# Expert routing of batches 2 to 7: turned on VectorE and moved by DMA, with TensorE, ScalarE and VectorE in a fixed order and the expert weights begun by GpSimd

## The chip, the cores and the metric

The kernel runs on one core of a Trainium2 chip. The metric is device time in microseconds (us) of one execution: 1364.11 us before, the median of three runs (1360.69 to 1366.95).

## The reference, cut to what matters

Eight batches of 256 tokens with 256 channels pass through two layers, all in float32. The changed part is the feed-forward of the first layer, a soft mixture of 8 experts with 128 slots each:

```python
xn = rmsnorm(x, norm_gamma);  sn = rmsnorm(slot_embeds, slot_norm_gamma)
logits   = einsum('bnd,esd->bnes', xn, sn)        # 256 tokens x 1024 slots per batch
dispatch = softmax(logits, axis=1)                # over the tokens
combine  = softmax(logits.reshape(b, n, e*s), axis=-1)   # over the slots
slots = einsum('bnd,bnes->besd', xn, dispatch)
h  = gelu(einsum('besd,edh->besh', slots, w1) + b1)      # 256 -> 1024
eo = einsum('besh,ehd->besd', h, w2) + b2                # 1024 -> 256
out = einsum('bmd,bnm->bnd', eo.reshape(b, e*s, 256), combine)
```

Before it stands a cross-attention with 16 heads of 16, behind it one with 16 heads of 64, and a gated channel mix ends the kernel.

## The kernel before

**Stages.** One program holds the first cross-attention (to about 286 us by the timeline), the expert phase (286.47 to 913.3), the second cross-attention and the channel mix. PSUM is shared out in three kinds of tile: `big`, two of 128x1024; `mm`, three of 128x512; `o`, one of 128x512.

**Experts.** The batches go in four groups of two (`experts(g)`, L951). An expert has eight pieces, one per 128 hidden columns: `up(e, hc)` (L957) is two matmuls into half of a `ph` tile, followed by a gelu on ScalarE (L976) into `ht`. The even and the odd piece share one `ph` tile. After each `up` a `down(e - 1, k)` (L979) of the expert before is issued: two matmuls of `ht` by `w2`, accumulated in `pe`. A matmul in float32 shows as two records on TensorE, so each `up` and each `down` is 4 records. The last `down` of an expert is followed on VectorE by the addition of `b2`, which leaves the expert's output in its `slots` tile (L993). `combine` (L1007) sums the eight outputs with the token weights `CT`, and scales by `rzn`.

**Routing.** While group g is in its experts, the routing of group g + 1 (`routing(g + 1)`, L804) and the combines of group g - 1 run as side pieces: a list `side`, from which one is taken after each odd piece from the tenth on (`n % 2 == 1 and n > 8`). For each batch there are

- `prepare`: normalised tokens `xh`, four transposes on TensorE, `xnT`;
- `by_token(t)`: logits `ln` of a half of the tokens by the 1024 slots (L832), the negated maximum on VectorE (L840), the exp with its sum on ScalarE into `en` (L843), and two copies of the logits into `lg` (L850);
- `turn_token(t)`: eight transposes of `en` on TensorE into `ptn` (L858), and copies into `CT` (L863);
- `by_slot(q)`: eight transposes of `lg` into `ls` in PSUM (L873), the maximum, four exps into `es` (L884), a multiplication by the reciprocal sums on GpSimd (L892);
- `turn_slot(q)`: eight transposes of `es` into `pts` (L902), copies into `dt`;
- `fill(q)`: `pf` = `xh` by `dt` (L914), scaled by `gam` into the `slots` tiles of the next group.

Routing of batches 0 and 1 stands in the first cross-attention (`routing0`) and works in its own way.

**Order.** The stages outside use helpers, `matmul` and `transpose` (L71 to L76), that hand the instruction to `tc.keep_in_program_order`; such instructions stand on their engine in the order of the code. In the expert phase plain `nc.tensor.matmul` and `nc.scalar.activation` are used, and a scheduler sets their order at build time by its own estimates.

**Weights.** `load_expert` (L217) issues `w1` (1 MB), `w2` (1 MB) and `b2` of one expert from SyncE, at the expert's first piece; two sets of tiles take turns (`moe_sets[e % 2]`). The first set is issued late in the first loads, at 30.30 us.

Of the kernel before, what the change touches and what calls it, by code (L numbers as in the profile page):

```python
# [14 lines left out]
P = 128  # L15
# [47 lines left out]
def kernel(ctx: ExitStack, tc: tile.TileContext, a: dict, out: bass.AP):  # L63
# [153 lines left out]
    def load_expert(to, e):  # L217
        nc.sync.dma_start(to["w1"], a["w1"][e].rearrange("(c p) f -> p c f", p=P))
        nc.sync.dma_start(to["w2"], a["w2"][e].rearrange("(c p) f -> p c f", p=P))
        nc.sync.dma_start(to["b2"], a["b2"][e].partition_broadcast(P))  # L220

    moe_sets = [moe_tiles(pr, 0)]
    with ExitStack() as l0:
# [550 lines left out]
        at(50, lambda: load_expert(set0, 0))  # L774
# [25 lines left out]
    with ExitStack() as l0f:  # L800
        pm = l0f.enter_context(tc.tile_pool(name="pm", bufs=2))
        moe_sets.append(moe_tiles(l0f.enter_context(tc.tile_pool(name="po", bufs=1)), 1))

        def routing(g):  # L804
# [7 lines left out]
            steps = []  # L812
            for bl in range(2):
# [3 lines left out]
                def prepare(b=b, st=st):  # L817
                    st["xh"] = normed(b, mv, scl, "moe", of=4)
                    pt = transposed(st["xh"], f"xm_{b}")
                    xnT = pm.tile([P, 2, S], F32, tag="xnT", name=f"xnT_{b}")  # L820
                    for c in range(2):
                        nc.vector.tensor_scalar(
                            xnT[:, c, :], pt[:, c, :], gam[:, c : c + 1], None, ALU.mult
                        )
                    st["xnT"] = xnT

                def by_token(t, b=b, bl=bl, st=st):

                    pl = ps_big(f"ln_{b}_{t}")
                    for m in range(2):  # L830
                        for c in range(2):
                            nc.tensor.matmul(  # L832
                                pl[:, m * 512 : (m + 1) * 512],
                                lhsT=st["xnT"][:, c, t * P : (t + 1) * P],
                                rhs=snT[:, c, m * 512 : (m + 1) * 512],
                                start=(c == 0),
                                stop=(c == 1),
                            )
                    nm = stat.tile([P, 4], F32, tag="nm", bufs=4, name=f"nmn_{b}_{t}")
                    nc.vector.tensor_reduce(nm[:, 0:1], pl, AX.X, ALU.max, negate=True)  # L840
                    en = pm.tile([P, 1024], F32, tag="em", bufs=4, name=f"en_{b}_{t}")
                    z = stat.tile([P, 4], F32, tag="zm", bufs=4, name=f"zn_{b}_{t}")
                    nc.scalar.activation(  # L843
                        en, pl, AF.Exp, bias=nm[:, 0:1], accum_out=z[:, 0:1]
                    )
                    nc.vector.reciprocal(rzn[:, 2 * bl + t : 2 * bl + t + 1], z[:, 0:1])
                    st[f"en{t}"] = en
                    for m in range(2):
                        lg = pm.tile([P, 512], F32, tag="lg", bufs=6, name=f"lg_{b}_{t}_{m}")
                        nc.vector.tensor_copy(lg, pl[:, m * 512 : (m + 1) * 512])  # L850
                        st[f"lg{t}{m}"] = lg

                def turn_token(t, b=b, bl=bl, st=st):
                    for m in range(2):
                        pt = ps_mm(f"ptn_{b}_{t}_{m}")
                        for i in range(4):
                            e = 4 * m + i
                            nc.tensor.transpose(  # L858
                                pt[:, i * P : (i + 1) * P],
                                st[f"en{t}"][:, e * P : (e + 1) * P],  # L860
                                ident,
                            )
                        nc.vector.tensor_copy(  # L863
                            CT[:, bl, 4 * m : 4 * m + 4, t * P : (t + 1) * P],
                            pt.rearrange("p (e n) -> p e n", e=4),
                        )

                def by_slot(q, b=b, st=st):

                    pl = ps_big(f"ls_{b}_{q}").rearrange("p (i n) -> p i n", i=4)  # L870
                    for i in range(4):
                        for t in range(2):
                            nc.tensor.transpose(  # L873
                                pl[:, i, t * P : (t + 1) * P],
                                st[f"lg{t}{q}"][:, i * P : (i + 1) * P],
                                ident,
                            )
                    nm = stat.tile([P, 4], F32, tag="nm", bufs=4, name=f"nms_{b}_{q}")
                    nc.vector.tensor_reduce(nm, pl, AX.X, ALU.max, negate=True)
                    es = pm.tile([P, 1024], F32, tag="em", bufs=4, name=f"es_{b}_{q}")  # L880
                    es = es.rearrange("p (i n) -> p i n", i=4)
                    z = stat.tile([P, 4], F32, tag="zm", bufs=4, name=f"zs_{b}_{q}")
                    for i in range(4):
                        nc.scalar.activation(  # L884
                            es[:, i, :],
                            pl[:, i, :],
                            AF.Exp,
                            bias=nm[:, i : i + 1],
                            accum_out=z[:, i : i + 1],
                        )  # L890
                    nc.vector.reciprocal(z, z)  # L891
                    nc.gpsimd.tensor_tensor(  # L892
                        es, es, z.unsqueeze(2).to_broadcast([P, 4, S]), ALU.mult
                    )
                    st[f"es{q}"] = es

                def turn_slot(q, b=b, st=st):
                    dt = pm.tile([P, 2, 512], F32, tag="dt", bufs=2, name=f"dt_{b}_{q}")
                    for t in range(2):
                        pt = ps_mm(f"pts_{b}_{q}_{t}")  # L900
                        for i in range(4):
                            nc.tensor.transpose(  # L902
                                pt[:, i * P : (i + 1) * P],
                                st[f"es{q}"][:, i, t * P : (t + 1) * P],
                                ident,
                            )
                        nc.vector.tensor_copy(dt[:, t, :], pt)
                    st[f"dt{q}"] = dt

                def fill(q, b=b, bl=bl, st=st):  # L910
                    for c in range(2):
                        pf = ps_mm(f"pf_{b}_{q}_{c}")
                        for t in range(2):
                            nc.tensor.matmul(  # L914
                                pf,
                                lhsT=st["xh"][:, t, c * P : (c + 1) * P],
                                rhs=st[f"dt{q}"][:, t, :],
                                start=(t == 0),
                                stop=(t == 1),
                            )  # L920
# [9 lines left out]
                steps.append([prepare])  # L930
                for t in range(2):
                    steps.append([lambda f=by_token, t=t: f(t), lambda f=turn_token, t=t: f(t)])
                for q in range(2):
                    steps.append(
                        [
                            lambda f=by_slot, q=q: f(q),
                            lambda f=turn_slot, q=q: f(q),
                            lambda f=fill, q=q: f(q),
                        ]
                    )  # L940
            pieces = []
            depth = max(len(s) for s in steps)
            for n in range(len(steps) + depth - 1):
                for k in range(depth):
                    if 0 <= n - k < len(steps) and k < len(steps[n - k]):
                        pieces.append(steps[n - k][k])
            return pieces, CT, rzn
# [3 lines left out]
        def experts(g):  # L951
# [5 lines left out]
            def up(e, hc):  # L957
                if hc == 0:
                    w = moe_sets[e % 2]
                    if g or e:  # L960
                        load_expert(w, e)
                    cur[e] = dict(w1=w["w1"], w2=w["w2"], b2=w["b2"], ht=[])
# [4 lines left out]
                for c in range(2):  # L967
                    nc.tensor.matmul(  # L968
# [7 lines left out]
                nc.scalar.activation(ht, ph, AF.Gelu, bias=b1[:, e, hc : hc + 1])  # L976
                c_["ht"].append(ht)

            def down(e, k):  # L979
# [3 lines left out]
                for hc in range(2 * (k % 4), 2 * (k % 4) + 2):  # L983
                    nc.tensor.matmul(  # L984
# [22 lines left out]
        def combine(g, bl, t, eos, CT, rzn):  # L1007
            pc = ps_mm(f"pc_{g}_{bl}_{t}")
            for e in range(E):
                nc.tensor.matmul(  # L1010
# [30 lines left out]
        for g in range(4):  # L1041
# [3 lines left out]
            if g < 3:  # L1045
                if g == 2:
                    moe_mean(3)
                    moe_scale([3])
                pieces, CT, rzn = routing(g + 1)
                side += pieces  # L1050
            for n, piece in enumerate(work_):
                piece()
                if n % 2 == 1 and n > 8 and side:
                    side.pop(0)()
# [464 lines left out]
```

## Time and profile before

| | |
|---|---|
| median of 3 runs | 1364.11 us |
| the profiled execution | 1366.39 us |
| its span in the trace | 1364.6 us |
| granted TensorE clock, mean | 0.989 |
| the expert phase | 286.47 to 913.3 us, 626.8 us |

The profile is one execution on the chip. PE is TensorE's matmul, PEld its weight load, DVE is VectorE, ACT is ScalarE, POOL is GpSimd, SP is SyncE, which here only issues DMAs. The first part of the page gives for each engine the busy microseconds, the share of the span and the number of instructions; matmuls are pipelined, and their ends are modelled, so busy times on PE overlap a little and start-to-start times are the better measure. The chain is followed back from the last instruction, at each step to what released it. A group is a line, an engine and an operation with its tiles (out<-in), a count, the busy time, the mean nanoseconds of one, and behind the last bar the idle time of the engine just before and what ended most of it. In the timeline a row has its start, its length, engine, line and operation, and in brackets the idle time before it. The duration of a merged row (x4, x8) covers all its instructions.

### The profile page before, as it was taken

How to read it: one execution, taken by the hardware profiler on the slowest of the kernel's cores; microseconds unless marked ns; L12 is line 12 of the kernel's file. 1: busy time of each engine (PE TensorE's matmuls, PEld its weight loads, DVE VectorE, ACT ScalarE, POOL GpSimd, SP SyncE). 2: the span in 40 equal slices, each digit the busy share in tenths (PEclk: the TensorE clock that was granted, in tenths of full speed). 3: DMA queues.
4: the chain of work that ended last, by engine and by line, in shares of the span. 5: the costliest groups of instructions: out<-in, count | busy, mean ns of one | idle time of the engine just before them, and what ended most of it. 6: DMA issues, size and time to landing. Idle time of an engine off the chain costs nothing.

```text
span 1364.6 us, 18968 instructions
## 1 busy us (share of the span) xinstructions
PE 1324.8 (97%) x7504; PEld 958.8 (70%) x7504; DVE 571.0 (42%) x1160; ACT 582.0 (43%) x1403; POOL 192.8 (14%) x142
## 2 busy tenths in 40 slices
PE   7998999899999999999999999999999999999998
PEld 3565565467678877778777788875666676677777
DVE  6577776523331133321333110015445444544565
ACT  2455444626342164522545222213536445444663
POOL 1000001101010000100001000002333323323433
PEclk8999998999999999999999999999999999999999
DMA  7100000023243324233233324450000000000001
GB/s 219 57 1 2 1 1 1 1 97 132 66 132 131 127 71 131 93 106 130 80 117 131 111 87 153 144 150 1 1 1 1 1 1 1 1 1 1 2 8 54
DMA packets 59128, 86.84 MB, mean 64 GB/s; under 512 B 3360, under 2 KB 49056, under 8 KB 59040
## 3 DMA queue, kind: packets, MB, share of 16 engines
q1 hardware_dynamic: 58464, 85.11, 19.2%
q8 instruction: 59, 0.97, 0.3%
q10 hardware_dynamic: 576, 0.52, 0.1%
q14 instruction: 29, 0.24, 0.1%
HBM read 83.53 MB, written 2.10 MB: 63 GB/s over the span
## 4 chain that ended last, share of the span: by engine, by line
PE 87%; ACT 6%; DVE 5%; issue 1%; DMA 0%; POOL 0%; ACTq 0%; SPq 0%; DVEq 0%; POOLq 0%
PE ph L968 16%; PE pe L984 16%; PE sc L73 8%; PE q L73 6%; PE o L73 5%; PE k L73 5%; PE po L73 5%; PE pc L1010 4%; PE pe L76 4%; PE v L73 4%; PE pf L914 3%; PE ln L832 3%; ACT ex L1222 2%; PE pf L73 1%; ACT ex L501 1%; DVE NM L490 1%
## 5 line engine op out<-in xcount | busy, mean ns | idle before, releaser
L976 ACT ACTIVATE ht<-ph,b 128x256 f32<-128x256 f32 x256 | 119.1, 473 | 372.1 <-PE ph L968 371.7
L968 PE MATMUL ph<-slots,w 128*128 128x256 f32 x1024 | 266.9, 384 | 0.9 <-ACT ht L976 0.2
L984 PE MATMUL pe<-w,ht 128*128 128x256 f32 x1024 | 263.3, 381 | 0.0
L968 PEld LDWEIGHTS ph<-slots,w 128*128 128x128 f32 x1024 | 182.3, 189 | 54.5 <-ACT ht L976 21.8
L984 PEld LDWEIGHTS pe<-w,ht 128*128 128x128 f32 x1024 | 192.0, 190 | 29.9 <-DVE slots L993 4.3
L1235 POOL TENSOR_TENSOR ex<-ex,rz 128x1024 f32<-128x1024 f32 x64 | 120.1, 1897 | 224.2 <-DVE rz L1233 214.0
L1222 ACT ACTIVATE ex<-sc,nm 128x256 f32<-128x256 f32 x256 | 117.2, 483 | 45.5 <-DVE nm L1217 45.5
L501 ACT ACTIVATE ex<-sc 128x512 f32<-128x512 f32 x128 | 74.7, 596 | 86.6 <-PE sc L73 76.1
L73 PE MATMUL sc<-KT,QT 17*128 17x256 f32 (+1 forms) x1024 | 105.3, 385 | 2.1 <-ACT QT L445 1.5
L490 DVE TENSOR_REDUCE NM<-sc 128x2 f32<-128x512 f32 x128 | 86.6, 687 | 41.4 <-PE sc L73 36.9
L993 DVE TENSOR_TENSOR slots<-pe,b 128x512 f32<-128x512 f32 x32 | 22.1, 691 | 185.4 <-PE pe L984 185.4
L73 PE MATMUL q<-xT,wq 128*128 128x256 f32 x384 | 94.8, 395 | 0.9 <-ACT V L1187 0.9
L73 PEld LDWEIGHTS sc<-KT,QT 17*128 17x128 f32 (+1 forms) x1024 | 77.4, 189 | 25.4 <-issue 15.9
L73 PEld LDWEIGHTS q<-xT,wq 128*128 128x128 f32 x384 | 70.9, 192 | 26.4 <-issue 12.9
L892 POOL TENSOR_TENSOR es<-es,zs 128x1024 f32<-128x1024 f32 x12 | 22.7, 1892 | 445.6 <-DVE zs L891 445.6
L1217 DVE TENSOR_REDUCE nm<-sc 128x4 f32<-128x1024 f32 x64 | 75.3, 1218 | 6.5 <-PE sc L73 2.8
L73 PE MATMUL po<-wo,ot 128*128 128x256 f32 x320 | 72.5, 382 | 0.0
L76 PE MATMUL pe<-ident,ex 128*128 128x128 f32 x512 | 69.9, 278 | 0.5 <-DVE xT L1137 0.4
L73 PEld LDWEIGHTS po<-wo,ot 128*128 128x128 f32 x320 | 60.1, 190 | 10.9 <-issue 3.2
L1251 ACT COPY et<-pe 128x512 f32<-128x512 f32 x64 | 37.0, 607 | 71.9 <-PE pe L76 71.5
L76 PEld LDWEIGHTS pe<-ident,ex 128*128 128x128 f32 x512 | 56.2, 140 | 14.0 <-issue 8.0
L73 PE MATMUL o<-et,V 128*64 128x256 f32 x512 | 62.8, 386 | 0.9 <-ACT ot L1270 0.9
(194 smaller groups left out, 1636.8 us busy)
## 6 DMA issues: line engine op xcount, KB each, us to landing
w<-in_w_dram SPq DMA_DIRECT2D x64, 1024.0 KB, 7.0
b<-in_b_dram SPq DMA_DIRECT2D x32, 128.0 KB, 6.8
x_sb<-in_x_dram SPq DMA_DIRECT2D x3, 512.0 KB, 7.3
ctx0T<-in_ctxT_dram SPq DMA_DIRECT2D x4, 256.0 KB, 8.4
ctx1T<-in_ctxT_dram SPq DMA_DIRECT2D x8, 128.0 KB, 6.9
se<-in_slots_dram SPq DMA_DIRECT2D x1, 1024.0 KB, 5.7
wq<-in_wq_dram SPq DMA_DIRECT2D x1, 1024.0 KB, 4.9
wo<-in_wo_dram SPq DMA_DIRECT2D x1, 1024.0 KB, 14.9
```

What stands on the lines that cost most here:

```text
L73: tc.keep_in_program_order(nc.tensor.matmul(out, lhsT=lhsT, rhs=rhs, start=start, stop=stop))
L76: tc.keep_in_program_order(nc.tensor.transpose(out, in_, ident))
L490: nc.vector.tensor_reduce(NMs[(2 * b + t // 2) % 2][:, qb, t, HD0 + 1 + 64 * i : 64 * i + 64 : 32], sc[i][:, :, 0, :], AX.X, ALU.max, nega ...
L501: nc.scalar.activation(ex[:, 2 - 2 * i : 4 - 2 * i, :], sc[1 - i][:, :, 1, :], AF.Exp)
L832: nc.tensor.matmul(pl[:, m * 512 : (m + 1) * 512], lhsT=st["xnT"][:, c, t * P : (t + 1) * P], rhs=snT[:, c, m * 512 : (m + 1) * 512], star ...
L968: nc.tensor.matmul(ph, lhsT=c_["w1"][:, c, hc * P : (hc + 1) * P], rhs=slots[e][:, c * 256 : (c + 1) * 256], start=(c == 0), stop=(c == 1),)
L976: nc.scalar.activation(ht, ph, AF.Gelu, bias=b1[:, e, hc : hc + 1])
L984: nc.tensor.matmul(c_["pe"][:, b, :], lhsT=c_["ht"][hc][:, b * SL : (b + 1) * SL], rhs=c_["w2"][:, hc, :], start=(hc == 0), stop=(hc == HI ...
L1010: nc.tensor.matmul(pc[:, :D], lhsT=CT[:, bl, e, t * P : (t + 1) * P], rhs=eos[e][:, bl, :], start=(e == 0), stop=(e == E - 1),)
L1217: nc.vector.tensor_reduce(nm, sc, AX.X, ALU.max, negate=True)
L1222: nc.scalar.activation(ex[:, i, qb, :], sc[:, i, qb, :], AF.Exp, bias=nm[:, i, qb : qb + 1], accum_out=z[:, i, qb : qb + 1],)
L1235: nc.gpsimd.tensor_tensor(ex, ex, rz.rearrange("p h q -> p (h q)").unsqueeze(2).to_broadcast([P, 4, S]), ALU.mult,)
```

## The change

For groups 1 to 3 (batches 2 to 7):

1. The 48 transposes of each batch on TensorE (`turn_token`, `by_slot`, `turn_slot`) and the 12 copies that follow them or save the logits are gone. In their place VectorE transposes 32x32 blocks (`turn`, and the two in `turn_slot`) into a tile of squares, `tk`, and `spread` moves the blocks to the partitions where they belong: 16 DMAs of 32 partitions (64 KB) on SyncE, three times per batch (logits into `ls`, `en` into `CT` in runs of 128 bytes, the dispatch weights into `dt`). `prepare`'s four transposes stay.
2. The softmax over the tokens reads and writes `ls` in SBUF, not PSUM.
3. The two exps over slots of a batch are issued together, behind the second half's maximum.
4. `tc.keep_in_program_order` (through `matmul` for TensorE) now holds the expert and routing matmuls, the gelus, the exps, the maxima of `by_slot` and the block transposes.
5. The side pieces have a written plan with gaps (`-`), and one is taken after each odd piece from the first on in groups 0 to 2. The four first steps of the next routing come ahead of the combines.
6. The weights are issued by GpSimd: `w2` and `b2` at the expert's first piece, `w1` of the next expert at its second. The first set is issued at the start.
7. `em`, `ls` and `dt` have fewer buffers.

```diff
-    def load_expert(to, e):
-        nc.sync.dma_start(to["w1"], ...)
-        nc.sync.dma_start(to["w2"], ...)
-        nc.sync.dma_start(to["b2"], ...)
+    def load_first(to, e):
+        nc.gpsimd.dma_start(to["w1"], ...)
+    def load_second(to, e):
+        nc.gpsimd.dma_start(to["w2"], ...)
+        nc.gpsimd.dma_start(to["b2"], ...)
...
+        def turn(tk, t, table):
+            for m in range(2):
+                square = nc.vector.transpose(
+                    tk[:, :, t, 4 * m : 4 * m + 4, :].rearrange("p k e x -> p e k x"),
+                    table[:, m * 512 : (m + 1) * 512].rearrange("p (e k x) -> p e k x", e=4, k=4),
+                )
+                tc.keep_in_program_order(square)
+
+        def spread(tk, to, rows="p t e x -> p t (e x)"):
+            for k in range(4):
+                for a in range(4):
+                    nc.sync.dma_start(
+                        to(32 * k, a), tk[32 * a : 32 * a + 32, k, :, :, :].rearrange(rows)
+                    )
...
+                    if t == 1:
+                        st["exp0"]()
+                        exp()
+                    if t == 0:
+                        st["tk_l"] = squares(f"l_{b}")
+                    turn(st["tk_l"], t, pl)
+                    if t == 1:
+                        ls = pm.tile([P, 8, E, 32], F32, tag="ls", bufs=1, name=f"ls_{b}")
+                        st["ls"] = ls
+                        spread(st["tk_l"], lambda k, a: ls[k : k + 32, a::4, :, :].rearrange("p t e x -> p t (e x)"))
...
-                def turn_token(t, b=b, bl=bl, st=st):
-                    for m in range(2):
-                        pt = ps_mm(f"ptn_{b}_{t}_{m}")
-                        for i in range(4):
-                            nc.tensor.transpose(pt[:, i * P : (i + 1) * P], ...)
-                        nc.vector.tensor_copy(CT[:, bl, 4 * m : 4 * m + 4, t * P : (t + 1) * P], ...)
+                def turn_token(b=b, bl=bl, st=st):
+                    tk = squares(f"n_{b}").rearrange("p k t e x -> p k (t e x)")
+                    tk = tk.rearrange("p k (e t x) -> p k t e x", t=2, x=32)
+                    for t in range(2):
+                        turn(tk, t, st[f"en{t}"])
+                    spread(tk.rearrange("p k t e x -> p k e t x"), ...)
...
-                    pl = ps_big(f"ls_{b}_{q}").rearrange("p (i n) -> p i n", i=4)
-                    for i in range(4):
-                        for t in range(2):
-                            nc.tensor.transpose(pl[:, i, t * P : (t + 1) * P], ...)
+                    ls = st["ls"][:, :, 4 * q : 4 * q + 4, :]
...
+            first = [piece(step) for step in ("P0", "T00", "T01", "P1")]
             pieces = []
+            for step in (
+                ("A0 - -" if g == 1 else "A0") + " S00 - S01 T10 - C0 T11 A1 - - F00 F01 S10 - S11 - C1 - - - F10 F11"
+            ).split():
+                pieces.append(piece(step))
+            return first, pieces, CT, rzn
...
+                if hc == 0 and n > 0:
+                    load_second(w, e)
+                if hc == 1 and n < 4 * E - 1:
+                    load_first(moe_sets[(e + 1) % 2], (e + 1) % E)
...
-                nc.scalar.activation(ht, ph, AF.Gelu, bias=b1[:, e, hc : hc + 1])
+                tc.keep_in_program_order(
+                    nc.scalar.activation(ht, ph, AF.Gelu, bias=b1[:, e, hc : hc + 1])
+                )
...
-                pieces, CT, rzn = routing(g + 1)
-                side += pieces
+                first, pieces, CT, rzn = routing(g + 1)
+                side = first + side + pieces
             for n, piece in enumerate(work_):
                 piece()
-                if n % 2 == 1 and n > 8 and side:
+                if n % 2 == 1 and (n > 8 or g < 3) and side:
                     side.pop(0)()
```

The letters of the plan are P `prepare`, T `by_token`, A `turn_token`, S `by_slot`, C `turn_slot`, F `fill`; the first digit is the batch of the pair, the second the half.

## Prediction

> **What bounds the kernel now.** I read the page first: engine busy times, then the chain that ended last.
>
> ```profile
> PE 1324.8 (97%) x7504; PEld 958.8 (70%) x7504; DVE 571.0 (42%) x1160; ACT 582.0 (43%) x1403; POOL 192.8 (14%) x142
> PE 87%; ACT 6%; DVE 5%; issue 1%; DMA 0%; POOL 0%; ACTq 0%; SPq 0%; DVEq 0%; POOLq 0%
> ```
>
> TensorE bounds it. The change lies in the expert phase, which by the timeline runs from 286.47 (first `ph` matmul) to 913.3, 626.8 us, with PE busy 625.95 at clock 1.00, DVE 152.9, ACT 232.4, POOL 22.8. So one microsecond of PE work saved is worth one microsecond, *unless the order opens a wait*. What PE waits for is in the groups, and the transposes that go are in the groups by form:
>
> ```profile
> L976 ACT ACTIVATE ht<-ph,b 128x256 f32<-128x256 f32 x256 | 119.1, 473 | 372.1 <-PE ph L968 371.7
> L968 PEld LDWEIGHTS ph<-slots,w 128*128 128x128 f32 x1024 | 182.3, 189 | 54.5 <-ACT ht L976 21.8
> L873 PE MATMUL ls<-ident,lg 128*128 128x128 f32 x96 | 13.4, 273 | 0.0
> L902 PE MATMUL pts<-ident,es 128*128 128x128 f32 x96 | 12.4, 273 | 0.0
> L858 PE MATMUL ptn<-ident,en 128*128 128x128 f32 x96 | 12.4, 273 | 0.0
> ```
>
> The one thing PE waits for is the gelu (L976): an odd `up` writes the second half of the PSUM tile whose first half the even gelu still reads. The timeline shows this beside an exp:
>
> ```profile
> 313.00 0.47 ACT L976 ACTIVATE ht<-ph,b 128x256 f32<-128x256 f32 x1 [2.17 <-PE ph L968]
> 313.49 1.28 ACT L843 ACT_TABLE_LOAD   x1
> 313.61 1.05 PE L968 MATMUL ph<-slots,w 128*128 128x256 f32 x4
> 314.50 1.03 PE L984 MATMUL pe<-w,ht 128*128 128x256 f32 x4
> 314.79 1.12 ACT L843 ACTIVATE en<-ln,nmn 128x1024 f32<-128x1024 f32 x1
> 315.36 1.04 PE L858 MATMUL ptn<-ident,en 128*128 128x128 f32 x8
> 315.80 0.19 ACT L843 ACTIVATION_READ_ACCUMULATOR en<-ln,nmn 128x1 f32 x1
> 316.01 1.28 ACT L976 ACT_TABLE_LOAD   x1
> 316.31 1.56 PE L984 MATMUL pe<-w,ht 128*128 128x256 f32 x6
> 317.31 0.47 ACT L976 ACTIVATE ht<-ph,b 128x256 f32<-128x256 f32 x1
> 317.83 0.73 PEld L968 LDWEIGHTS ph<-slots,w 128*128 128x128 f32 x4 [0.36 <-ACT ht L976]
> ```
>
> ACT is away from gelus for 3.84 us (table, exp, table). The scheduler fills that time with eight transposes and six `down` matmuls moved forward, and PE loses 0.36. The exps over tokens take longer:
>
> ```profile
> 322.34 0.47 ACT L976 ACTIVATE ht<-ph,b 128x256 f32<-128x256 f32 x1 [1.05 <-PE ph L968]
> 322.83 1.28 ACT L884 ACT_TABLE_LOAD   x1
> ...
> 326.07 1.28 ACT L976 ACT_TABLE_LOAD   x1
> 327.37 0.84 ACT L976 ACTIVATE ht<-ph,b 128x256 f32<-128x256 f32 x2
> ```
>
> From 322.81 to 327.37 no gelu starts: 4.56 us.
>
> **What goes.** 288 transposes. Eight in a row take 0.87 to 0.95 us start to start (315.36 to 316.31 is the longer), so 31.3 to 34.2; the rows' busy sum is 38.2, but busy times overlap. I take 31.3. With 0.217 us per `ph`/`pe` record (four in 0.867), 0.43 per 512-wide record and 3.46 per combine, the phase holds 615.5 of PE work; so 626.8 - 615.5 = 11.3 are waits now. About 0.27 per expert, 8.6 over 32, is the even-gelu pattern away from any exp. It stays; the other 2.7 are counted anew below. Work left: 584.2.
>
> **What the fixed order adds.** In the built program's order PE is even `up`, `down`, odd `up`, `down`, side piece, with nothing moved across, and ACT goes gelu(odd), exps, gelu(next even). The piece S (exps over tokens) has no PE work any more. After the slot boundary PE has `up` and `down`, 1.73 us; the gelu before the exps ended 0.13 ahead of the boundary, so the next ends at -0.13 + 4.56 + 0.47 = 4.90 and PE resumes at 4.95. **Stall 3.2 us, times 12 = 38.4.** Where an S's data come late it is longer: S00 of groups 1 and 2 waits some 1.6 us for the moved logits (twice), in group 0 the reduce of S00 stands behind expert 0's add (+1.0) and that of S10 likewise (+2.25); 6.45 in all. S: 44.9.
>
> The piece T has 3.43 us of PE work per token half. Both exps now run after the second half's reduce (1.22 us) at 3.43 + 0.2 + 1.22 = 4.85; the second exp ends at 6.1, the table load at 7.4, the gelu at 7.9; PE is ready at 5.17. Stall 2.8, five times 13.9. The sixth, in group 0's first expert, has no `down`s beside it: 2.0 for the gelu table (a load at 287.57 and a gelu, less one `up`), 0.78 in each of two pieces whose gelu has no `down` to hide behind, and 2.8 + 0.87 for the missing `down`: 7.2. T: 21.1. In before each T filled itself with transposes. Six table pairs are saved on ACT, which I count inside these sums.
>
> The square root of the next layer's statistics takes a table pair too, some 2.15 each for three groups and 1.7 for the last scale: 8.2.
>
> Phase: 584.2 + 8.6 + 44.9 + 21.1 + 8.2 = **667.0, 40.2 more.**
>
> **What moves off PE.** 60 block transposes on DVE: the nearest rows are 0.714 us for 128x512 from PSUM and 0.436 for 128x256 from SBUF, and 12 of the 60 are 128x1024, so 51 to 55 us on an engine busy 153 of 627; 72 copies (0.64 each, 46 us) go. Hidden by PE, except where one stands ahead of an S reduce (the lateness above).
>
> 288 DMAs from SBUF to SBUF, 64 KB each, on SP. SP's issue costs
>
> ```profile
> 24.12 4.10 SPq L280 DMA_DIRECT2D wo<-in_wo_dram  x8
> ```
>
> 0.51 us each, 8.2 for a spread's sixteen, plus 2.1 to land (those eight landed after 2.3): 10.2 us. No trace here has SBUF to SBUF with 128-byte runs; records of 256 bytes take 18 ns, so 512 runs over 16 engines are 0.58 per DMA, about the issue. Below: 8.2, the issue alone. Above: lane j+8 waits for lane j, two landings of the slowest kind on the page, 14.9 each: 30. I take 10.2, nearest to the 32 KB row. Between first exps and S00 in group 0 stand 5.6 us more than that, between the slot softmax's spread and its fill (C0 to F00) 8, for C1 to F10 0.4 in group 0 and 6 later, and the CT spread must land within 14 before the piece queued behind it asks. So at 10.2 it costs only the 1.6 counted.
>
> Weights leave SP for POOL, in two parts, each a piece earlier or later. A 1 MB load lands 7.0 us after its issue (page); first use is 7 and 8 pieces of 1.73 us later, 12.1 and 13.9. POOL has two 1.9 us multiplications per batch in the phase ahead of them: no cost. The first set moves from 30.3 us to about 4 us, where 2.2 MB share the DMA with the first loads (slice one: 219 GB/s); 2.2 MB at that rate would be 10 us, and the chain there has 0.6 us of slack. Bounds 0 and 10; I take 1, since the loads ahead were issued first.
>
> [...]
>
> Sum: the profiled execution took 1366.4 (span 1364.6); + 40.2 + 1 = 1407.6. The median of the three runs is 2.3 below it: **1405 us**.
>
> **Rivals.**
> - *Faster, 1330 to 1345.* The even gelu isn't late, because the exps start before the slot boundary or the odd `up` isn't held by the shared tile: then an exp block costs under 1 us and the transposes are gained: 1364 - 31.3 - 2.7 + 0 to 15. For it: PE waits only 11 us today with twelve more table pairs. Against: today's cover is `down`s and transposes that the scheduler moved, and the fixed order moves none. It decides if the stall per block (12 S, 6 T, 4 square roots) is under (31.3 + 2.7)/22, about 1.5 us, instead of 3.
> - *No change, about 1368.* Stalls at S as worked out but nothing late, none at T and the square root, whose matmuls cover them as now: 584.2 + 8.6 + 38.4 = 631.2, 4.4 more. For it: T has 3.43 us of matmuls of its own. Against: both exps stand behind them.
> - *Much slower, 1420 to 1450.* Spreads take 20 us instead of 10: S00 then comes some 5 late in group 0 and 10 in the others, the fills 2 to 6: about 6 per batch, 36. It decides from 16 us per spread; speaking for it, each has 512 runs of 128 bytes.
>
> **How the numbers follow.** Forecast 0.70 (1380 to 1425, the stall per block between 2 and 4 us), faster 0.13, no change 0.07, much slower 0.10. The range 1368 to 1435 leaves out the faster case and the far end of the slower. Measurement tells 0.5% (6.8 us) from no change: faster 0.13, same 0.07, slower 0.80.
>
> **What would show it.** No `ptn`, `ls`, `pts` groups on PE; L968's load idle behind ACT up from 22 to some 95 us; PE empty for 3 us after each block of four exps, in the timeline; the phase about 667 long; chain share of ACT up by 4 to 5 points. Wrong if the phase is under 627, if PE's idle is put down to a DMA (the spreads), or if the stages before 286 and after the phase moved.

## The result, and the profile after

The changed kernel took 1452.62 us (median of four, 1446.23 to 1458.04) against 1362.72 for the kernel before (1360.69 to 1366.95): ratio 1.0654, 95% interval 1.0601 to 1.0707. It is slower, as forecast, but by 89.9 us and not by 41; the time lies above the range, which ended at 1435.

These are lines of the page of the changed kernel: busy time of the engines, the granted clock in 40 slices, the chain by engine, and the groups of the `up`s (their matmuls and their weight loads).

```profile
PE 1332.4 (92%) x7216; PEld 956.2 (66%) x7216; DVE 569.2 (39%) x1148; ACT 570.2 (39%) x1391; POOL 262.7 (18%) x238
PEclk9999999998989998989989899999999999999999
PE 74%; ACT 10%; DVE 6%; DMA 5%; SPq 3%; issue 2%; POOL 0%; DVEq 0%; ACTq 0%; POOLq 0%
L73 PE MATMUL ph<-slots,w 128*128 128x256 f32 x1024 | 289.4, 408 | 71.8 <-ACT ht L1021 71.7
L73 PEld LDWEIGHTS ph<-slots,w 128*128 128x128 f32 x1024 | 198.1, 202 | 130.7 <-ACT ht L1021 94.8
```

The clock row and the same group of matmuls in the kernel before:

```profile
PEclk8999998999999999999999999999999999999999
L968 PE MATMUL ph<-slots,w 128*128 128x256 f32 x1024 | 266.9, 384 | 0.9 <-ACT ht L976 0.2
```

PE has 288 instructions fewer and is yet busy for 7.6 us more. That is the line to stop at: the work shrank by 31 us, so what is left must have run slower. The mean of one `ph` record rose from 384 to 408 ns, and the clock row shows dips between slices 10 and 23, in the expert phase, where before it was level. The wait for the gelu is where the prediction put it: PEld's idle time behind ACT is 94.8 us, and ACT's share of the chain went from 6% to 10%.

What one block of exps does is in the timeline of the changed kernel, PE alone (start, length, operation, and in brackets the idle time before):

```profile
414.63 1.03 PE L73 MATMUL ph<-slots,w 128*128 128x256 f32 x4
415.50 1.03 PE L73 MATMUL pe<-w,ht 128*128 128x256 f32 x4
419.73 2.07 PE L73 MATMUL ph<-slots,w 128*128 128x256 f32 x4 [3.21 <-ACT ht L1021]
421.60 1.91 PE L73 MATMUL pe<-w,ht 128*128 128x256 f32 x4
423.30 1.91 PE L73 MATMUL ph<-slots,w 128*128 128x256 f32 x4
425.01 1.46 PE L73 MATMUL pe<-w,ht 128*128 128x256 f32 x4
426.31 1.03 PE L73 MATMUL ph<-slots,w 128*128 128x256 f32 x4
```

The pause is 3.21 us, as long as forecast (3.37 in the account below, which counts from the end of the work and not from the modelled end of the record). But behind it the same four records start 1.70 us apart (421.60 to 423.30) instead of 0.87 (414.63 to 415.50), for some 6.5 us. The table of windows gives the reason; its column behind POOL is the granted clock, 0.50 in the middle row (called half clock from here on):

```profile
412.00:415.00 3.00, 3.00 (x15) 2.63 (x14) 0.00 (x0) 1.42 (x3) 0.00 (x0) 0.96 0.00 0
420.00:425.00 5.00, 5.00 (x12) 3.94 (x13) 0.00 (x0) 0.47 (x1) 0.07 (x1) 0.50 0.00 0
427.00:430.00 3.00, 3.00 (x15) 2.40 (x14) 1.77 (x2) 0.95 (x2) 2.21 (x3) 1.00 0.22 30
```

**The account of the phase.** For every PE record I took the time to the next one. At full clock 0.217 us of it is work for a 128x256 record, 0.433 for a 512-wide one, 0.108 for a transpose (the medians from start to start in the expert phase of before, at clock 1.00, are 0.216, 0.429 and 0.109); what a stretch at clock 0.5 adds to that is put under "clock", the rest under "wait". The phase runs from the first `ph` to the last combine.

| kernel | phase | work | wait | clock | median of all runs | ratio to before, 95% |
|---|---|---|---|---|---|---|
| before | 626.7 | 616.2 | 10.4 | 0.0 | 1362.7 | |
| changed | 714.1 | 585.0 | 87.6 | 41.5 | 1452.6 | 1.0654 (1.0601 to 1.0707) |
| e1_filler | 689.1 | 637.0 | 46.3 | 5.7 | 1429.1 | 1.049 (1.0452 to 1.0528) |
| e3_weights_sp | 704.6 | 585.0 | 85.9 | 33.7 | 1441.4 | 1.0581 (1.0537 to 1.0625) |
| e4_ph_tiles | 625.8 | 585.0 | 32.0 | 8.8 | 1370.0 | 1.0056 (1.0032 to 1.008) |
| e5_before_fixed | 766.7 | 616.2 | 104.6 | 45.9 | 1504.3 | 1.1042 (1.0999 to 1.1086) |
| e2_free_order | 615.9 | 585.0 | 27.6 | 3.3 | 1357.3 | 0.9963 (0.9951 to 0.9976) |
| e7_plan | 641.6 | 585.0 | 47.6 | 9.0 | 1382.4 | 1.0146 (1.0115 to 1.0177) |
| e8_plan_tiles | 606.5 | 585.0 | 17.3 | 4.2 | 1349.3 | 0.9906 (0.9888 to 0.9925) |
| e10_room | 626.8 | 585.0 | 36.4 | 5.4 | 1367.5 | 1.0032 (1.0016 to 1.0049) |
| e9_best | 605.2 | 585.0 | 17.0 | 3.1 | 1349.0 | 0.9903 (0.9882 to 0.9923) |
| e11_before_tiles | 621.5 | 616.2 | 5.2 | 0.0 | 1356.2 | 0.995 (0.9937 to 0.9963) |
| e12_free_tiles | 616.6 | 585.0 | 24.1 | 7.5 | 1358.6 | 0.9968 (0.9945 to 0.9991) |
| e13_last | 590.6 | 585.0 | 5.6 | 0.0 | 1333.1 | 0.9789 (0.9762 to 0.9816) |

The prediction had 584.2 of work and 82.8 of waits; 585.0 and 87.6 came. The phase was 47.1 us longer than forecast: 41.5 of half clock, 4.8 more of waits and 0.8 of work.

### The profile page after: what moved, and what is told of

Same layout as the page of the kernel before. It is cut to its first block, busy times and chain, and to the rows that moved or that the text cites. A ratio compares the mean times of both kernels' runs of the same rounds, so it can differ in the third digit from the quotient of the medians.

```text
span 1452.6 us, 18782 instructions
## 1 busy us (share of the span) xinstructions
PE 1332.4 (92%) x7216; PEld 956.2 (66%) x7216; DVE 569.2 (39%) x1148; ACT 570.2 (39%) x1391; POOL 262.7 (18%) x238
## 4 chain that ended last, share of the span: by engine, by line
PE 74%; ACT 10%; DVE 6%; DMA 5%; SPq 3%; issue 2%; POOL 0%; DVEq 0%; ACTq 0%; POOLq 0%
PE ph L73 14%; PE pe L73 13%; PE sc L73 7%; PE q L73 6%; PE o L73 5%; PE po L73 5%; PE k L73 4%; PE pe L76 4%; PE v L73 3%; PE ln L73 3%; SPq L823 3%; PE pf L73 3%; PE pc L73 3%; ACT L1021 2%; ACT ex L1268 2%
## 5 line engine op out<-in xcount | busy, mean ns | idle before, releaser
L73 PE MATMUL ph<-slots,w 128*128 128x256 f32 x1024 | 289.4, 408 | 71.8 <-ACT ht L1021 71.7
L73 PEld LDWEIGHTS ph<-slots,w 128*128 128x128 f32 x1024 | 198.1, 202 | 130.7 <-ACT ht L1021 94.8
L73 PE MATMUL pe<-w,ht 128*128 128x256 f32 x1024 | 279.9, 399 | 0.8 <-DVE slots L1039 0.8
L73 PEld LDWEIGHTS pe<-w,ht 128*128 128x128 f32 x1024 | 205.1, 202 | 38.5 <-DVE slots L1039 7.3
L218 POOL DMA_DIRECT2D w<-in_w_dram x32 | 23.1, 722 | 445.8 <-PE ph L73 409.6
```

What stands on the lines that cost most here:

```text
L73: tc.keep_in_program_order(nc.tensor.matmul(out, lhsT=lhsT, rhs=rhs, start=start, stop=stop))
L218: nc.gpsimd.dma_start(to["w1"], a["w1"][e].rearrange("(c p) f -> p c f", p=P))
```

## The experiments

The theory after the result: the fixed order opens pauses on TensorE at each block of exps, and a pause costs about half as much again (41.5 us on 87.6 in the changed kernel), because the matmuls behind it run at half clock. Rivals: the clock falls for another reason (loads begun by GpSimd, the DMAs from SBUF to SBUF), or the moved routing, not the order, is what costs.

**e1_filler: the pauses filled with useless work.**

```diff
+                if step[0] == "S" or step[0] == "T" and step[2] == "1":
+                    def filled(n=7 if step[0] == "S" else 6):
+                        f(*args)
+                        spare = ps_mm(f"spare_{g}_{step}")
+                        for _ in range(n):
+                            matmul(spare[:, :256], lhsT=snT[:, 0, :P], rhs=snT[:, 0, :256],
+                                   start=True, stop=True)
+                    return filled
```

> The changed kernel with useless matmuls of 128x256 (7 behind each exp piece over tokens, 6 behind the second exp piece over slots) written to a spare PSUM tile, so that TensorE works where it now waits for the gelu. Nothing else changes. In the changed kernel the expert phase is 714.1 us: 585.0 of matmuls at full clock, 87.6 of waits, 41.5 because matmuls after a wait run at a granted clock of 0.5. Theory 'pauses': the clock falls because TensorE paused, so the filled waits (some 50 us) stay as long as they were but the clock loss falls to about 10: 1415 to 1425 us. Rival 'traffic': the clock falls for another reason that comes with the change (loads begun by GpSimd, or the DMAs from SBUF to SBUF); then the clock loss stays near 41 and the time near 1452.

1429.1 us. 52 us of matmuls that compute nothing were added, and the kernel became 23.5 us faster. The clock loss fell from 41.5 to 5.7 with all the traffic in place, so the rival "traffic" falls. The time is 4 us above the expected range, since waits of 1.20 us stayed behind most blocks. The timeline of e1_filler shows why:

```profile
334.80 2.32 PE L73 MATMUL spare_S<-snT 128*128 128x256 f32 x10
...
336.95 1.03 PE L73 MATMUL ph<-slots,w 128*128 128x256 f32 x4
...
337.82 1.03 PE L73 MATMUL pe<-w,ht 128*128 128x256 f32 x4
338.06 1.28 ACT L1036 ACT_TABLE_LOAD   x1 [0.87 <-PE ph L73]
339.36 0.47 ACT L1036 ACTIVATE ht<-ph,b 128x256 f32<-128x256 f32 x1
...
339.88 1.13 PE L73 MATMUL ph<-slots,w 128*128 128x256 f32 x4 [1.04 <-ACT ht L1036]
```

The gelu's table load at 338.06 waited for the `up` of 336.95, as the gelu itself does. So the useless work ahead of that `up`, 2.32 us from 334.80 on, delayed the table load too.

**e3_weights_sp: weights back on SyncE.**

```diff
-        nc.gpsimd.dma_start(to["w1"], ...)
+        nc.sync.dma_start(to["w1"], ...)
```

(and so for `w2` and `b2`.)

> The changed kernel with the expert weights issued by SyncE instead of GpSimd, at the same places in the code. Theory 'pauses': the queue of the weights has no part in it, 1445 to 1460 us; a little more if loads that wait for their buffer hold up the DMAs of the routing behind them in SyncE's queue. Rival 'traffic': loads from GpSimd are what lowers the clock or comes late; then 1410 to 1425.

1441.4 us, 11 us less than the changed kernel and just below the range of the theory, nowhere near the rival's. The intervals of the two ratios overlap. The waits are the same within 2 us (85.9 and 87.6), the rest is the clock (33.7 and 41.5). Where the weights are issued decides little; whether it is worth some 10 us is not settled by two runs.

**e4_ph_tiles: a PSUM tile for each `up`.**

```diff
-                if hc % 2 == 0:
-                    c_["ph"] = ps_mm(f"ph_{g}_{e}_{hc}").rearrange("p (i n) -> p i n", i=2)
-                ph = c_["ph"][:, hc % 2, :]
+                ph = ps_mm(f"ph_{g}_{e}_{hc}")[:, :256]
```

> The changed kernel with a PSUM tile of its own for each up (still three in turn) instead of one for the even and the odd. TensorE then has three ups and three downs (5.2 us) before it needs the first gelu behind a block of exps (4.95 us after the slot boundary). Theory 'pauses, by the shared tile': nearly all waits of 2.8 to 3.4 us go, and with them the half clock; left are the late logits (some 3 us, twice or three times) and the first expert: phase 600 to 615, 1335 to 1355 us. Rival 'ScalarE is late whatever the tile': the wait only moves to the next up, 1430 to 1452.

1370.0 us: 82.6 us back by an edit that replaces three lines with one. In e4_ph_tiles the group of `ph` waits 16.8 us for ACT in place of 71.8, and the mean of a record is again 383 ns:

```profile
L73 PE MATMUL ph<-slots,w 128*128 128x256 f32 x1024 | 265.9, 383 | 16.8 <-ACT ht L1019 16.8
```

The pauses of 2.8 and 3.4 us are all gone; the rival falls. It ended 15 us above the expected range, because the data that come late cost more than I gave them: 5.4 and 5.9 us at the first exps over tokens of two groups, 2.6 to 3.9 us at three fills, and the half clock behind them.

**e5_before_fixed: the fixed order alone, in the kernel before.**

```diff
-                            nc.tensor.matmul(
+                            matmul(
...
-                        nc.scalar.activation(
+                        tc.keep_in_program_order(nc.scalar.activation(
```

(so for all matmuls, transposes, gelus and exps of the phase.)

> The kernel before with one part of the change alone: matmuls, transposes, gelus and exps of the expert phase are kept in the order of the code. The transposes stay on TensorE, the side pieces where they were, the weights on SyncE. Theory 'fixed order': every block of exps makes TensorE wait, 12 of 3.4 to 4.7 us and 12 of 2.8 to 4.0, and the clock halves behind each: 75 to 104 + 35 to 50, so 1475 to 1515 us. Rival 'the moved routing costs': the fixed order alone is harmless, 1360 to 1385.

1504.3 us, in the range. No work was moved, no DMA added, and 104.6 us of waits and 45.9 of clock appeared. The timeline of e5_before_fixed at one block (with most rows left out):

```profile
328.72 1.28 ACT L884 ACT_TABLE_LOAD   x1
...
328.83 1.04 PE L873 MATMUL ls<-ident,lg 128*128 128x128 f32 x8
...
330.57 1.03 PE L73 MATMUL pe<-w,ht 128*128 128x256 f32 x4
...
333.12 1.28 ACT L976 ACT_TABLE_LOAD   x1
...
334.41 0.47 ACT L976 ACTIVATE ht<-ph,b 128x256 f32<-128x256 f32 x1
...
334.94 1.90 PE L73 MATMUL ph<-slots,w 128*128 128x256 f32 x4 [3.34 <-ACT ht L976]
...
336.64 1.91 PE L73 MATMUL pe<-w,ht 128*128 128x256 f32 x4
```

The eight transposes at 328.83 stand ahead of the exps and cover nothing; in the kernel before the scheduler put `down`s in the gap. The same half clock follows, without any load from GpSimd.

**e2_free_order: the change without the fixed order on TensorE and ScalarE.** The edit is the reverse of that of e5_before_fixed, made in the changed kernel.

> The changed kernel without the fixed order on TensorE and ScalarE in the expert phase (matmuls, transposes, gelus and exps left to the scheduler; the block transposes and maxima on VectorE stay in order). Routing on VectorE and by DMA, plan and weights as in the changed kernel. Theory 'the fixed order leaves the pauses open': the scheduler moves downs into the blocks of exps as it did in before; waits 25 to 40 instead of 87.6, clock loss under 10, so phase 615 to 635 and 1350 to 1375 us. Rival 'without the transposes the scheduler has nothing to fill with': waits stay over 60 and the time over 1400.

1357.3 us: 95 us of the change undone by its order, and 0.4% faster than before. The scheduler puts `down`s into the blocks again, eight records at a time, though there are no transposes to use. The phase still has 27.6 us of waits. Some 8.5 of them are for data that a DMA brought late: 3.3 and 0.7 at two fills, 3.4 and 1.2 at two `down`s for an expert's weights. The others are for gelus and additions, none over 2.0 us.

**e7_plan, e8_plan_tiles, e10_room: the rest of the waits.** In the trace of the changed kernel the first exps over tokens come 3.4 us later than the others while groups 1 and 2 are in their experts. VectorE's timeline tells why (the same view of SP has the sixteen `ls` DMAs from 524.78 to 534.95):

```profile
522.57 0.48 DVE L1064 SCALAR_TENSOR_TENSOR x_sb<-pc,rzn,x_sb 128x256 f32<-128x256 f32 x1 [2.76 <-PE pc L73]
...
523.30 0.21 DVE L875 RECIPROCAL rzn<-zn 128x1 f32<-128x1 f32 x2
523.42 1.29 DVE L814 STREAM_TRANSPOSE tk_l<-ln 128x512 f32<-128x512 f32 x2
...
536.51 1.22 DVE L909 TENSOR_REDUCE nms<-ls 128x4 f32<-128x1024 f32 x1 [5.96 <-DMA ls<-tk_l]
```

The reciprocals at 523.30 write `rzn`, of which there are two; the new one takes the place of the one that the last combine (522.57) still reads. The block transposes and the DMAs of the logits are queued behind them. e7_plan has a third `rzn` and a new plan:

```diff
-            rzn = stat.tile([P, 4], F32, tag="rzn", bufs=2, name=f"rzn_{g}")
+            rzn = stat.tile([P, 4], F32, tag="rzn", bufs=3, name=f"rzn_{g}")
...
+                "P0 T00 P1 - T01 - A0 - - - S00+S01+T10 - - C0 - - - - T11+F000 - - - - - "
+                "S10+S11+F001+F010+F011 - - C1 A1 - - F10 F11"
+                if g == 1
+                else "P0 T00 P1 - T01+K0 - - - S00+S01+K1+K2 K3 C0 A0 - - T10 T11+F000 - - A1 - - - "
+                "S10+S11+F001+F010+F011 - C1 - - - - - K4+F10 F11"
```

(K0 to K3 are the combines, K4 the statistics, a third digit of F is one of its two halves; `zm` has three buffers instead of four to make room. e7_plan and e10_room change the tile and the plan together, and the long waits at the first exps of groups 1 and 2 are gone in both; what the tile alone is worth is not shown.)

> The changed kernel with another plan of side pieces and one tile of rzn more (so that the reciprocals of the next group's tokens need not wait for the last combine): exps over tokens of a batch in one block, with matmuls of a combine, of the logits or of a fill behind them in the same slot to cover them, fills later behind their DMAs. The even and the odd up still share a tile. Theory 'pauses': nearly every block is covered, about 1.0 to 1.2 us a block stays, because the gelu's table load waits for the up behind the cover; phase 605 to 625, 1345 to 1365 us. Rival 'the blocks cost their time on ScalarE however TensorE is ordered': over 1400.

1382.4 us, 70 us less than the changed kernel but 17 above the expected range. Most blocks are covered, with 1.20 us left each as in e1_filler; a fill during group 0 waited 10.3 us for its DMAs, which I had not counted.

> The plan of e7_plan together with the tile for each up of e4_ph_tiles. Theory 'pauses': both covers together leave the first expert's waits and little else, waits under 12, no half clock in the phase: 592 to 602, 1332 to 1345 us, faster than before by the transposes' 31 us less what is left. Rival 'late DMAs': fills still wait for their DMAs by 3 to 6 us a group and pull the clock down, 1350 to 1365.

1349.3 us, between the two, at the rival's end. While groups 1 and 2 run there is no wait over 0.6 us; in group 0, two fills waited 2.3 and 8.8 us.

e10_room is e4_ph_tiles with the third `rzn`, S00 among the combines, and five empty slots ahead of the last fills.

> e4_ph_tiles with the late data mended and nothing else: one more tile of rzn, the first exps over tokens among the combines instead of behind them, and two more empty slots ahead of the last fills. Theory 'late data': the 5.4 and 5.9 us waits at the first exps of groups 1 and 2 and the 2.6 to 3.9 us waits of the last fills go, with the 8.8 of clock loss: phase 598 to 610, 1338 to 1352 us. Rival: the data are as late as before, only elsewhere, 1360 to 1370.

1367.5 us: a miss, the rival holds. S00 comes in time, but the first fills of two groups wait 8.7 and 9.6 us; that the DMAs of A0 and C0 now meet in SyncE's queue is my reading of it.

**e9_best, e11_before_tiles, e12_free_tiles.** e9_best is e8_plan_tiles with the first group's plan "P0 T00 P1 T01 - - - - S00+S01 - C0 A0 - - T10 T11 F00 F01 A1 - - S10+S11 - C1 - - - - - F10 F11"; the other two are the edit of e4_ph_tiles in before and in e2_free_order.

> e8_plan_tiles with the plan of the first group made like that of the others (the steps that start DMAs six slots ahead of the steps that need them). In e8_plan_tiles the two waits of the first group for its fills, 2.3 and 8.8 us, and the 4.2 of half clock behind them are most of what was left. Theory: they go; phase 585 to 596, 1333 to 1343 us. Rival: the DMAs of the routing are late again in another place and the time stays at 1347 to 1352.

1349.0 us, the rival again: the waits for the fills went, and one of 9.5 us came at the first exps. The timeline of e9_best:

```profile
307.77 11.81 SPq L823 DMA_DIRECT2D ls<-tk_l  x16
...
316.91 0.72 POOL L218 DMA_DIRECT2D w<-in_w_dram  x1 [15.69 <-PE ph L73]
...
317.77 0.92 POOL L221 DMA_DIRECT2D w<-in_w_dram  x1
...
326.89 1.22 DVE L909 TENSOR_REDUCE nms<-ls 128x4 f32<-128x1024 f32 x1 [8.70 <-DMA ls<-tk_l]
```

The last of the sixteen was issued by 319.6 and the logits were there at 326.9, 7.3 us later, where the median of these DMAs lands after 2.0. The two loads of 1 MB that POOL issued began just before the end of the sixteen. In the packets of this trace no packet of SyncE's queue starts between 318.5 and 321.8 us, while 212 of GpSimd's with 0.87 MB do, and the last of SyncE's come at 326.1. That the loads held up the small DMAs is the reading that fits this; no run took the loads away.

> The kernel before with a PSUM tile of its own for each up, nothing else. Its expert phase has 10.4 us of waits, 8.5 of them in front of an up. Theory: the shared tile is what makes those; 1355 to 1361 us. Rival: the scheduler has already hidden the tile, and the third tile is missed by the transposes, 1362 to 1372.

1356.2 us, as the theory had it: the tile is worth 6 us to the kernel before, whose waits halve (10.4 to 5.2).

> e2_free_order with a PSUM tile of its own for each up. Theory: the scheduler's order and the tile cover the same pauses, so the tile adds only what e2_free_order still waits for, some 10 to 15 of its 27.6 us: 1342 to 1352 us. Rival: nothing left for the tile to cover, 1353 to 1360.

1358.6 us, the rival: on top of the scheduler the tile adds nothing that can be measured. The runs lie between 1350.6 and 1367.7.

**e13_last: the first group's plan shifted once more**, to "P0 T00 P1 T01 - - A0 - - - S00 S01+T10 - C0 T11 - - - - F00 F01 - S10 S11 - C1 A1 - - - - F10 F11".

> e9_best with the first group's plan shifted again: the first exps over tokens two slots later, since in e9_best the last logits landed 7 us after the last of their sixteen DMAs was issued (the weights of an expert were issued at the same time), and the fills seven slots behind the DMAs they need. Theory: the waits of 9.5 and 3.7 us and the half clock of 3.1 go; phase 587 to 597, 1332 to 1341 us. Rival: the collision of the routing's DMAs with the weights moves elsewhere, 1345 to 1352.

1333.1 us, 2.1% faster than the kernel before (95% interval 1.8 to 2.4%), and 23 us faster than before with the same tile (e11_before_tiles). Its phase is 30.9 us shorter than that one's, and 616.2 - 585.0 = 31.2 is what the 288 transposes cost. The medians are only 23 us apart because the phase itself starts later, at 288.0 us against 281.9. In the windows of e13_last the phase has the clock at 1.00 throughout, and PE's wait for the gelu is 2.3 us:

```profile
288.00:879.00 591.00, 587.68 (x2522) 474.81 (x2521) 150.58 (x322) 208.66 (x419) 89.35 (x106) 1.00 0.54 156
```

```profile
L73 PE MATMUL ph<-slots,w 128*128 128x256 f32 x1024 | 262.4, 379 | 2.3 <-ACT ht L1023 2.3
```

So the gain that the change was good for exists, and its own order gave it back three times over.

## Why the prediction was wrong in size

- **What goes (31.3): right.** Work fell by 31.2.
- **Stalls at the exps over tokens (44.9): right in kind, 50.2 measured.** Ten of the twelve are near the working: 3.37 to 4.05, and 5.38 (forecast 5.45) for one whose maximum stands behind an expert's addition. The two behind the combines were 6.8 and not 4.8: I gave the late logits 1.6 us and did not see that, by the reading of e7_plan above, the reciprocals wait for `rzn`.
- **Stalls at the logits (21.1): 2.78 five times and 7.2 in the first expert, to a tenth.** Square root: 8.2 forecast, 4.4 measured. That the waits came so near in all (82.8 and 87.6) is in part luck: S was 5.3 short and one fill 3.6, against 3.8 too much here.
- **The step that failed** is the term "Stall 3.2 us, times 12 = 38.4", and the stalls at T with it: it takes the wait for the whole price and every later matmul at the clock of the phase before, 1.00. In its place 87.6 us of waits brought 41.5 us of half clock. The term was not mis-sized, it was missing. It could have been looked for: the clock row of the page of before dips in its seventh slice, and in its timeline five short pauses of PE, 0.24 to 1.03 us and 2.65 together, stand between 210.5 and 217, just ahead of a stretch at 0.5 from 217.6 to 224.4. In the expert phases of the fourteen traces the stretches at 0.5 last 3.4, 6.8 or 10.2 us and once 13.7. Of 56 pauses above 3.0 us, 55 had half clock behind them, and of 36 between 2.0 and 3.0 us, 25.
- **The DMAs of the routing:** landing 2.0 us was right as the median (the slowest took 9.9), the issue was not: sixteen take 10.2 to 15.2 us on SyncE, 0.64 to 0.95 each, against 0.51 in the row I used. Only the DMAs into `CT` have runs of 128 bytes, and these landed after 2.1 us in the median. From its first issue to its last landing a spread took 11.6 to 19.3 us, and the margin of C1 to F10 broke: one fill waited 3.56 us, for which I had counted nothing.
- **Weights by GpSimd:** within the phase no cost that shows. They land 6.6 us after issue (7.0 before), and e3_weights_sp has the same waits within 2 us (85.9 and 87.6).
- **The first set of weights: 1 us forecast, about 4.5 measured, and hidden by luck.** The reason given, that the loads ahead were issued first, does not hold for all of them: GpSimd issues the weights at 4.09 and 4.95 us, and SyncE's loads from 5.57 us on are issued behind them (`wq` landed 9.7 us after its issue, 3.4 before). PE waits 6.02 us for the first `QT` instead of 1.52, and its 65th record starts at 28.2 us instead of 23.7 (22.9 in e3_weights_sp, which issues this set at 30.49). The phase starts at 286.3 us all the same (286.5 before), since the first stage happened to lose 10.2 us to half clock and not 15.4; e5_before_fixed and e11_before_tiles, which begin as before does, lost 12.0 and 10.2.
- **Of the rivals,** the upper one had nearly the time but not the cause: its late DMAs are a few microseconds of the 89.9.

## What to carry to other kernels

Price a pause of the engine that bounds the kernel with what it does to the clock: here half clock added 41.5 us to 87.6 of waits in the changed kernel and 45.9 to 104.6 in e5_before_fixed, and in the fourteen traces it followed 55 of the 56 pauses above 3.0 us. Before fixing an order by hand, list each block in which another engine is away (here a change of function table, 1.28 us; four exps with a change before and one behind, 4.56 us; a reduction, 1.22 us) and name the matmuls that stand behind it; if a buffer shared by two steps makes them wait, split the buffer first (82.6 us in e4_ph_tiles). Start DMAs several slots ahead of the step that needs them, and ask what else is issued at that moment.

## What the runs showed of the hardware

- **Pauses and half clock.** Over the expert phases of all fourteen traces: of 104 pauses between 0.4 and 2.0 us, 5 were followed by half clock within 9 us, four of them in e12_free_tiles, each within 4 us of another pause; of 36 between 2.0 and 3.0 us, 25; of 56 above 3.0 us, 55.
- **Useless work paid in e1_filler:** 52 us of it saved 35.8 us of clock loss and 41.3 of waits, so the phase became 25.0 us shorter.
- **Times spread more in two kernels with half clock in the phase.** The ten runs of e12_free_tiles and the four of the changed kernel spread over 17 and 12 us, four of the five runs of e13_last over 0.7 us (1332.67 to 1333.33; the fifth took 1337.33). That the pauses cause the spread is not shown: the two runs of e1_filler, with 5.7 us of clock loss, lie 1.2 us apart.
- **The table load before an activation waited for the operands of that activation** (338.06 in e1_filler), so 1.28 us stood behind the wait instead of beside it. Not every one did so: that at 328.72 in e5_before_fixed ran 1.16 us ahead of its exp.
